# Half the products in the way back from the spectrum, x with its second half reversed throughout, and another order of first loads, fold and gates

## The chip, the cores and the metric

The kernel runs on one core of a Trainium2 chip. TensorE (PE) multiplies matrices, VectorE (DVE), ScalarE (ACT) and GpSimd (POOL) work on tiles element by element, and SyncE (SP) issues the DMAs. The metric is the device time of one launch in microseconds (us), median of several runs. Everything is float32, and each float32 matrix product stands in the profile as two records of PE.

## What is computed

Two layers of a gated cross-attention stack, for x and ctx of shape (8, 256, 1024):

```
x += tanh(g_xattn[0]) * autocorrelation(layernorm(x), ctx, ctx)      # 8 heads, top 11 lags
x += tanh(g_ffn[0])   * (LN(x) @ W.T + b + LoRA of a gated rank)     # ranks 8, 16, 32, 64
x += tanh(g_xattn[1]) * GQA(LN(x), ctx, ctx, mask)                   # 32 query, 8 key heads, rope
x += tanh(g_ffn[1])   * (LN(x) @ W1.T + b1 + 0.5 * Fourier update)

autocorrelation: corr = ifft(fft(q) * conj(fft(k))).real   over the 256 positions, per channel
  w, lag = top_k(corr, 11); w = softmax(w)
  out[t] = sum_i w_i * v[min(lag_i + t, 255)]
```

The values of the autocorrelation are thus another correlation, of v with the sparse weights, in which positions past the end count as the last one. The kernel does it with transforms of length 512 for v, 256 for the scores.

## The kernel before

The eight samples go in two passes of four (`NPASS`, `BP`). A pass holds its x as eight tiles of 128 positions by 1024 (`xt`) and takes them through all four parts; out is stored tile by tile at the end of `fourier_ffn`. The larger matrix products are made of seven products of half blocks in place of eight (`SEVEN`, `left_operands`, `right_operands`, `combine`), from operands that are sums and differences of blocks; in pass 0 they are made on chip and stored to DRAM (`wk_d`, `w0_d`, `w1_d` and others), later they are loaded.

Autocorrelation (`autocorrelation`) goes over 8 steps of a pass, a sample and half of the channels (512) each. `loads` brings the context in halves, its last row (`end`), and the second half of x reversed (`xr`, a second copy of the input). `sums` normalizes x and forms sums and differences of the position pairs (n, 255 - n), for x (`qe`, `qo`) and context (`ke`, `ko`). `normalize` forms the statistics; those of the second half are turned around by a product with a reversing matrix (`flip`, L406), since `xr` is reversed and `xt` is not. `turn` interleaves one step's forward half with the previous step's backward half: cosine and sine products (`dft`, L416), products of spectra on VectorE and their sums on GpSimd (`products`), the correlation (L563), the lags on VectorE (`lags`), and, for the previous step, the transforms of the weights, `er`, `ei` (even frequencies), `odr`, `odi` (odd), and `back` (L528): for each of the two position tiles four products with `inv2` added up in one PSUM tile, `po`, then one `residual` (L364) on VectorE that adds `tg * po` to x. The pool of `pt` and `po` (`ps_out`) has one buffer.

Between these stand steps of another generator (`beside`, run by `fill`): `keys_values` makes keys and values of the pass from ctx, 56 steps of four products for each 512 rows, and in pass 0 `fold_last_layer` then adds the Fourier update to W1. Eight steps run before the autocorrelation begins, 104 within, what is left after. Their big tiles come from two groups of seven buffers of 4 KB per partition, `ga` and `gb`: in pass 0 `ga` holds key and value weights (later all of the fold's tiles), `gb` the context (later, with `ga`, the weight `w0`). In `keys_values`, for the first 512 rows, `weight` loads four raw blocks at a unit's start, makes the sums (first unit on VectorE, the rest on GpSimd through `Short`) and stores four of them after the unit.

The fold multiplies the coefficients by a Fourier matrix (L295), and then in four rounds loads two raw W1 tiles (`w1in`), adds the update (L313, L320), forms the sums (`t12`, `t47`) and stores all to `w1_d`.

`lora_ffn` takes pairs of tiles: `prepare` normalizes and transposes a tile, multiplies it by the LoRA and gate matrix `ag` (L616), picks the rank in small VectorE operations, and transposes the result `xa` (`px`, L637); `left` forms the operands; `project` runs the seven products for the previous pair. `attention` and `fourier_ffn` follow.

The instructions of all engines are put in order ahead of time by a scheduler, which goes by the order of the program and by when it takes inputs and buffers to be free; each engine then works in its fixed order. SP's DMAs wait in that order too.

## Time and profile before

| | us |
|---|---|
| median of 3 runs (3470.31 to 3475.52) | 3472.91 |
| profiled execution | 3473.84 |
| its span | 3471.7 |
| VectorE busy | 2209.5 |
| GpSimd busy | 1412.9 |
| mean granted clock of TensorE | 0.984 |

The span is from the first to the last instruction. A line of the timeline has the start, the duration, engine, source line, operation, output and inputs, the count, and in brackets the idle time before it and what ended it. A wait line has the waiting engine and line, what it waited for, the total in us, how often and the longest. DMA issues are SP's.

### The profile page before, as it was taken

The page shows a single profiled execution, that of the slowest core. Times are in us where ns is not written, and L with a number is a line of the kernel's source. Part 1 is how long each engine was busy: PE and PEld are TensorE (multiplying, and loading weights), DVE is VectorE, ACT ScalarE, POOL GpSimd, SP SyncE. Part 2 cuts the span into 40 slices and gives each one's busy share as a digit, 9 for nine tenths or more (in the row PEclk, how much of TensorE's full clock was granted, in tenths as well). Part 3 has the DMA queues.
Part 4 walks back from the last instruction along what each step waited for, and adds up shares of the span by engine and source line. Part 5 has one row for each costly group of instructions (what it writes and reads, how often), then busy time and mean ns, then how long its engine had stood idle before and what let it go on. Part 6 is the DMA issues. An engine that isn't in the chain of part 4 may idle for free. (4 is left out here: it accounts for less than half of the span.)

```text
span 3471.7 us, 37174 instructions
## 1 busy us (share of the span) xinstructions
PE 3372.3 (97%) x12888; PEld 2303.4 (66%) x12888; DVE 2209.5 (64%) x4149; ACT 860.4 (25%) x2065; POOL 1412.9 (41%) x1259
## 2 busy tenths in 40 slices
PE   6999979999999999999999999999999999999999
PEld 4666634876777677676456666467776777777654
DVE  7667455777777766666548674456666666666662
ACT  2222101222223232223113321113222222222220
POOL 4655213244344334434545552224344344344343
PEclk8999979999999999999999999999999999999999
DMA  6343551433333333344153434043333333333411
GB/s 234 130 142 113 180 179 54 167 138 134 136 136 120 126 119 121 123 134 138 55 201 119 151 112 158 0 158 112 119 117 123 115 121 120 118 124 121 152 49 49
DMA packets 164169, 435.66 MB, mean 125 GB/s; under 512 B 21604, under 2 KB 56676, under 8 KB 163982
## 3 DMA queue, kind: packets, MB, share of 16 engines
q1 hardware_dynamic: 163982, 433.29, 37.4%
q8 instruction: 102, 1.67, 0.2%
q14 instruction: 85, 0.70, 0.1%
HBM read 354.59 MB, written 78.64 MB: 125 GB/s over the span
## 5 line engine op out<-in xcount | busy, mean ns | idle before, releaser
L699 POOL TENSOR_TENSOR qT<-rope,rope 128x512 f32<-128x512 f32 x128 | 170.0, 1328 | 865.4 <-DVE rope L698 865.4
L928 PE MATMUL po<-wo,oT 128*128 128x512 f32 x960 | 432.1, 593 | 0.0
L899 PE MATMUL ps_q<-xn,wq 128*128 128x256 f32 x1920 | 428.9, 379 | 0.0
L364 DVE SCALAR_TENSOR_TENSOR x<-po,tg,x 128x512 f32<-128x512 f32 x360 | 258.4, 745 | 231.9 <-PE po L928 70.6
L899 PEld LDWEIGHTS ps_q<-xn,wq 128*128 128x128 f32 x1920 | 364.8, 190 | 50.5 <-PE po L669 0.5
L961 ACT ACTIVATE s<-s,nmx 128x256 f32<-128x256 f32 x512 | 256.0, 501 | 275.7 <-DVE nmx L958 275.2
L956 DVE COPY_PREDICATED s<-keep,ps_s 128x512 f32<-128x512 uint8 x256 | 186.1, 730 | 182.3 <-PE ps_s L947 178.8
L928 PEld LDWEIGHTS po<-wo,oT 128*128 128x128 f32 x960 | 177.4, 190 | 175.6 <-issue 170.5
L928 PE MATMUL po<-wo,oS 128*128 128x512 f32 x640 | 287.7, 592 | 0.3 <-DVE x L364 0.3
L899 PE MATMUL ps_q<-xn_t,wq 128*128 128x256 f32 x1280 | 285.6, 379 | 0.0
L988 ACT COPY wT<-pt 128x512 f32<-128x512 f32 x256 | 138.0, 590 | 516.3 <-PE pt L982 516.3
L899 PEld LDWEIGHTS ps_q<-xn_t,wq 128*128 128x128 f32 x1280 | 243.2, 190 | 33.1
L993 PE MATMUL av<-wT,v 128*128 128x256 f32 x1024 | 247.1, 384 | 2.9 <-ACT wT L988 2.9
L947 PE MATMUL ps_s<-kT,qT 128*128 128x256 f32 x1024 | 248.3, 380 | 0.0
L993 PEld LDWEIGHTS av<-wT,v 128*128 128x128 f32 x1024 | 191.9, 190 | 78.0 <-issue 44.0
L970 DVE TENSOR_SCALAR s<-s,tot 128x256 f32<-128x256 f32 x512 | 219.6, 469 | 7.7
L955 POOL MEMSET s<- 128x512 f32 x256 | 129.8, 526 | 222.9 <-PE pt L982 221.1
L252 POOL TENSOR_TENSOR x<-x,part 128x512 f32<-128x512 f32 x80 | 115.0, 1437 | 255.1 <-ACT part L251 255.1
L696 DVE TENSOR_TENSOR rope<-c,tab 128x512 f32<-128x512 f32 x160 | 116.4, 728 | 154.0 <-POOL c L234 147.3
L928 PEld LDWEIGHTS po<-wo,oS 128*128 128x128 f32 x640 | 118.9, 190 | 136.7 <-issue 128.9
L947 PEld LDWEIGHTS ps_s<-kT,qT 128*128 128x128 f32 x1024 | 191.9, 190 | 25.5 <-DVE x L364 0.5
L958 DVE TENSOR_REDUCE nmx<-s 128x2 f32<-128x512 f32 x256 | 175.0, 685 | 8.3
(260 smaller groups left out, 5673.5 us busy)
## 6 DMA issues: line engine op xcount, KB each, us to landing
wq<-in_wq_dram SPq DMA_DIRECT2D x104, 512.0 KB, 3.4
wo<-in_wo_dram SPq DMA_DIRECT2D x104, 512.0 KB, 3.4
wq<-wq_d SPq DMA_DIRECT2D x96, 512.0 KB, 3.3
wo<-wo_d SPq DMA_DIRECT2D x96, 512.0 KB, 3.2
w<-w_d SPq DMA_DIRECT2D x36, 512.0 KB, 4.8
wk<-in_wk_dram SPq DMA_DIRECT2D x26, 512.0 KB, 5.1
wv<-in_wv_dram SPq DMA_DIRECT2D x26, 512.0 KB, 3.9
wk<-wk_d SPq DMA_DIRECT2D x24, 512.0 KB, 4.4
```

Of the source, the lines that this page charges most:

```text
L364: nc.vector.scalar_tensor_tensor(xs, ps, g, xs, ALU.mult, ALU.add)
L699: nc.gpsimd.tensor_add(dst, t0, t1)
L899: nc.tensor.matmul(ps[:, l, :], wops[r][:, l, c, :], xo[r][:, c, :], start=(c == 0), stop=(c == KH - 1),)
L928: nc.tensor.matmul(po, ops[r][:, h, t * P : (t + 1) * P], wops[r][:, h, :], start=(h == 0), stop=(h == 1),)
L947: nc.tensor.matmul(ps[:, t, :], qT[i, n][:, l, t * P : (t + 1) * P], kT[:, n * S : (n + 1) * S], start=True, stop=True,)
L955: nc.gpsimd.memset(s, MASKED)
L956: nc.vector.copy_predicated(s, keep[b], ps)
L958: nc.vector.tensor_reduce(nmx, s, AX.X, ALU.max, negate=True)
L961: nc.scalar.activation(s[:, t, :], s[:, t, :], AF.Exp, bias=nmx[:, t : t + 1], accum_out=tot[:, t : t + 1],)
L970: nc.vector.tensor_scalar(s[:, t, :], s[:, t, :], tot[:, t : t + 1], None, ALU.mult)
L988: nc.scalar.copy(wT[i], pt)
L993: nc.tensor.matmul(av[:, i, :], kv[step][1][:, n * 2 + c, :], wT[i][:, c, :], start=(c == 0), stop=(c == 1),)
```

## The change

- x comes in, and stays, with its second half of positions reversed in every sample; so do the mask's rows and the query side's rope table (`tab_q`). `xr`, `flip` and the turned statistics go. On the way out the second tile of each sample is scattered to its rows by an indirect DMA of GpSimd, through row numbers `rows`; the first is stored by SP as before.
- Position n's pair is now 255 - n for x, but the context is paired with one shift (n - 1 with 255 - n, `front`), so that the value correlation has a part that is the same for both positions of a pair and one that is opposite. `back(0)` makes the shared part from `er` and `odi`, `back(1)` the opposite one from `ei` and `odr`: two products each; each result goes to both tiles, the second time with `tg` or `ntg`. The context transforms have own matrices (`KCE` and so on), and one more product (`NYQ`) for each step.
- Loads: matrices, first context, `inv`, `inv2` and two x tiles come ahead of the other six x tiles (`late`). In pass 0, 1 + 6 steps of `keys_values` run ahead of the statistics and 7 after them; in pass 1, 1 + 4 and 3.
- `raw_weight` loads the next unit's blocks after the fourth of the seven products of a unit, just after its stores; the second `wk` unit's sums go to VectorE.
- The fold takes `w1in` from the other group (`gb`). `w0` is asked for after `ag` and `bl`.
- In `lora_ffn` the gates' transposes (`turned`) come after two steps of the previous projection; `xa` and `xaT` have four buffers.

```diff
@@ load_constants
         nc.sync.dma_start(tab, a["rope"])
+        nc.sync.dma_start(tab_q, a["rope_q"])
+        nc.sync.dma_start(rows, a["rows"])
@@ fold_last_layer
-                wt.append(big_tile(group, [2, HALF], "w1in"))
+                wt.append(big_tile(wt_group, [2, HALF], "w1in"))
@@ autocorrelation
-        mats = c1.tile([P, 4, P], F32, name="mats")
+        mats = c1.tile([P, 9, P], F32, name="mats")
         nc.sync.dma_start(mats, a["dft"])
-        inv = c1.tile([P, 2, S], F32, name="inv")
-        nc.sync.dma_start(inv, a["dft_inv"])
-        inv2 = c1.tile([P, 4, S], F32, name="inv2")
-        nc.sync.dma_start(inv2, a["lag_inv"])
-        flip = c1.tile([P, P], F32, name="flip")
-        nc.sync.dma_start(flip, a["flip"])
...
-            ps = ps_cor.tile([P, S], F32, tag="cor", name="ps_turn")
-            nc.tensor.matmul(ps[:, 0 : n * 2], flip, flat, start=True, stop=True)
...
             for b in range(n):
-                norms[b0 + b] = lin[:, b * 2, :], turned[:, b, :]
+                norms[b0 + b] = lin[:, b * 2, :], lin[:, b * 2 + 1, :]
-
-        normalize(0, 1)
...
-                kr_ps, ki_ps = dft(CE, ke), dft(SE, ko)
+                kr_ps, ki_ps = dft((KCE, ke)), dft((KSE, ko), (NYQ, ke))
...
-                vr_ps, vi_ps = dft(CO, ko), dft(SO, ke)
+                vr_ps, vi_ps = dft((KCO, ko)), dft((KSO, ke))
...
                     po = ps_out.tile([P, HALF], F32, tag="out", name="po")
-                    for k, sp in enumerate((er, ei, odr, odi)):
-                        nc.tensor.matmul(
-                            po, inv2[:, k, l * P : (l + 1) * P], sp, start=(k == 0), stop=(k == 3)
-                        )
-                    residual(b_tiles[l][:, b_cols], po, tg_x[0])
+                    for i, (k, sp) in enumerate(((0, er), (3, odi)) if l == 0 else ((1, ei), (2, odr))):
+                        nc.tensor.matmul(po, inv2[:, k, :], sp, start=(i == 0), stop=(i == 1))
+                    residual(b_tiles[0][:, b_cols], po, tg_x[0])
+                    residual(b_tiles[1][:, b_cols], po, ntg_x[0] if l else tg_x[0])
                     fill(1)
...
-        this, before = sums(*loads(order[0])), None
+        first = loads(order[0])
+        inv = c1.tile([P, 2, S], F32, name="inv")
+        nc.sync.dma_start(inv, a["dft_inv"])
+        inv2 = c1.tile([P, 4, P], F32, name="inv2")
+        nc.sync.dma_start(inv2, a["lag_inv"])
+        late()
+        fill(6 if p == 0 else 4)
+        normalize(0, 1)
+        this, before = sums(*first), None
+        fill(7 if p == 0 else 3)
@@ lora_ffn
+                return xnT, xa
+
+            def turned(xnT, xa):
                 px = ps_s.tile([R0 + 1, P], F32, tag="s", name="px")
                 nc.tensor.transpose(px, xa, ident)
...
-                got = left(m, prepare(m * 2, norm), prepare(m * 2 + 1, norm))
-                if pending is not None:
-                    project(*pending)
-                elif make_w0:
+                got = [prepare(m * 2 + i, norm) for i in range(2)]
+                steps = project(*pending) if pending else iter(())
+                for _ in range(2):
+                    next(steps, None)
+                got = left(m, *(turned(*x) for x in got))
+                if pending is None and make_w0:
                     w0.update(make_w0())
+                for _ in steps:
+                    pass
@@ keys_values
+        def raw_weight(kind, u):
             w = [[big_tile(gw, [KC * P], f"{kind}_{i}{k}") for k in range(2)] for i in range(2)]
...
+        def made_weight(kind, u, w):
             s = [big_tile(gw, [KC * P], f"{kind}_s{i}") for i in (1, 2, 4)]
             if cops:
-                ops = left_operands(Short(nc.gpsimd), w, *s)
+                eng = Short(nc.gpsimd if kind == "wv" else nc.vector)
+                return left_operands(eng, w, *s)
...
+                if n == 0 and r == SEVEN[3]:
+                    for d, k in zip(kept, (5, 7, 6, 3)):
+                        nc.sync.dma_start(d, ops[k])
+                    if u < 3:
+                        coming = raw_weight(("wk", "wv")[(u + 1) // 2], (u + 1) % 2)
                 yield
-            for d, t in later:
-                nc.sync.dma_start(d, t)
-            later.clear()
@@ attention, queries
-                        rope(qT[done[1]], done[0], tab[:, 0, :], tab[:, 1, :], w1)
+                        rope(qT[done[1]], done[0], tab_q[:, 0, :], tab_q[:, 1, :], w1)
@@ fourier_ffn
-                for i in range(2):
-                    r0 = (p * TT + m * 2 + i) * P
-                    nc.sync.dma_start(out[r0 : r0 + P, :], xt[m * 2 + i])
+                b = p * BP + m
+                nc.sync.dma_start(out[b * S : b * S + P, :], xt[m * 2])
+                nc.gpsimd.indirect_dma_start(
+                    out,
+                    bass.IndirectOffsetOnAxis(ap=rows[:, b : b + 1], axis=0),
+                    xt[m * 2 + 1],
+                    None,
+                )
@@ flamingo_kernel
-                    yield from fold_last_layer(ga, (kw1, ps_kv))
+                    yield from fold_last_layer((ga, gb), (kw1, ps_kv))
...
-            for t in range(TT):
-                r0 = (p * TT + t) * P
-                nc.sync.dma_start(xt[t], a["x"][r0 : r0 + P, :])
-            for _ in range(7):
-                next(steps)
+            load_x(range(2))
...
-        if p == 0:
-            w0, make_w0 = {}, ffn_weight(nc.vector, (gb, ga), lambda k, j: a["w0"][k, j])
...
                 nc.sync.dma_start(bl, a["bl"])
+                if p == 0:
+                    w0, make_w0 = {}, ffn_weight(nc.vector, (gb, ga), lambda k, j: a["w0"][k, j])
@@ _layout
-        "x": i["x"].reshape(B * S, D),
-        "xr": i["x"][:, : P - 1 : -1].reshape(B * P, D),
-        "ctx": turned(i["ctx_4096"]).reshape(B * S, D),
+        "x": turned(i["x"]).reshape(B * S, D),
+        "ctx": paired.reshape(B * S, D),
```

## The prediction

> **What bounds it now.** I read the busy shares first, then the busy time by stretch, then who waited for whom, then the timeline at the longest waits.
>
> ```profile
> PE 3372.3 (97%) x12888; PEld 2303.4 (66%) x12888; DVE 2209.5 (64%) x4149; ACT 860.4 (25%) x2065; POOL 1412.9 (41%) x1259
> ```
>
> TensorE (PE) sets the end: only 99 us of 3471.7 are without a matmul. So a removed matmul counts in full wherever PE has no gap, and a removed gap counts too. The busy time by stretch (columns: width, then busy us and instructions of PE, weight loads, VectorE, ScalarE, GpSimd; granted clock; DMA share; GB/s) shows where gaps lie:
>
> ```profile
> 40.00:200.00 160.00, 132.76 (x456) 90.92 (x457) 106.72 (x242) 44.90 (x82) 105.80 (x80) 0.89 0.46 155
> 200.00:410.00 210.00, 208.52 (x804) 148.05 (x803) 134.03 (x343) 55.32 (x100) 101.55 (x81) 1.00 0.41 131
> 410.00:500.00 90.00, 72.44 (x200) 31.38 (x199) 49.91 (x103) 6.48 (x14) 5.59 (x4) 0.77 0.67 231
> ```
>
> PE is full at clock 1.00 in 200 to 410 us (autocorrelation of pass 0), and loses time at the start and in the fold (410 to 500), partly to a lower clock. PE's waits (total us, times, longest):
>
> ```profile
> PE acc L313 <- DVE w1in L320: 15.1, 3, 6.3
> PE px L637 <- DVE xa L635: 12.0, 7, 1.8
> PE ps_k L774 <- POOL wk_s L152: 9.4, 1, 9.4
> ...
> PE pa L616 <- DMA ag<-in_ag_dram: 6.8, 1, 6.8
> ...
> PE ps_turn L406 <- ACT cor L566: 4.0, 1, 4.0
> ```
>
> Nearly half of the 99 us stand in these five lines, and each of the five instructions is touched by the change.
>
> **Reverse transform: products removed.** The chain has the price of a product:
>
> ```profile
> 2099.96 3.43 PE po L532 x8
> ```
>
> Eight records are the four products of one `back`: each float32 product is two records, so 0.86 us. A turn drops from 8 products to 4, and gains one (the Nyquist row, `NYQ`). With 16 turns (2 passes x 4 samples x 2 column halves): 16 x 3 x 0.86 = 41.3. The flip products of the statistics go too (8 records, 1.5 us busy, hidden in part): 0.7. Together **-42**.
>
> VectorE gets two more `residual` per turn: 32 x 0.745 = 23.8 us (mean of its group). Its cover is the PE-bound stretch, where it is busy 134 of 210 us, so nothing is charged; with the cover gone it would cost up to 23.8. But order matters. Turn five of pass 0:
>
> ```profile
> 281.27 1.72 POOL L438 TENSOR_TENSOR odi<-ma,mb 128x512 f32<-128x512 f32 x1
> 281.61 1.02 PE L532 MATMUL po<-odr,inv 128*128 128x512 f32 x2
> 283.05 1.12 PE L532 MATMUL po<-odi,inv 128*128 128x512 f32 x2 [0.43 <-POOL odi L438]
> 288.40 0.74 DVE L364 SCALAR_TENSOR_TENSOR x<-po,tg,x 128x512 f32<-128x512 f32 x1
> 289.20 1.13 PE L532 MATMUL po<-re,inv 128*128 128x512 f32 x2
> ```
>
> `odi`, the last thing GpSimd makes, was the fourth product; in the new `back(0)` it is the second, 1.7 us sooner. Here it ends at 282.99 and would be wanted at 280.75: 2.2 us of wait. The same subtraction in all 16 turns gives 12.7 (three turns of each pass with 0.9 to 2.4, the rest near nothing), 0.7 of it there already: +12. PE is in order, so the fill and next transposes queue behind. `po` has one buffer, now held for two residuals: in the same turn the second `back` started 0.06 us after the residual, so 0.74 more lands on PE, in four turns or so: +2. I take **+14**; ends 0 (other products are placed between) and +25.
>
> **First loads.** Pass 0 now loads two x tiles, the matrices and the first context before the other six x tiles, runs 14 key steps instead of 8 ahead of the first turn, loads the second raw key weights in the middle of the previous unit, and makes them on VectorE instead of GpSimd. Moved on SP's queue: six x loads behind `cn`, `end`, `inv`, `inv2`; four stores and four raw loads before the next `cn`, the last raw loads holding SP until a key product is done. `tab_q` and `rows` are two small loads more; the `xr` loads (16 x 256 KB) go. Stretch 40 to 200 holds 119 us of work at back-to-back spacing (0.43 us per record of 512 columns, in proportion to columns), so 41 are lost. Removable: the wait on `wk_s` 9.4 and the half-speed records behind it 1.9 (8 records 3.78, elsewhere 1.89); `ke` 3.8 and half-speed transforms behind 2.6; `re`, `im`, `kn`, the raw load 6.2 and 1.5 behind. That is 25. What stands in the way is VectorE: 106.7 busy, plus 8 half-operations of 0.68 (5.4) and 3 us of residuals, is 115 in a stretch that would be 160 - 25 - 10 = 125. GpSimd falls from 105.8 to about 94. At 92% VectorE would be the next thing late, with key products waiting on its evictions; the two `ps_v` waits (3.3 and 5.5, both on VectorE) stay. I take **-17**; ends -3 and -25.
>
> Here a rule weighs. The Trainium skill, TensorE: Matmul & The Clock Gate, section Part 1: The HAM clock gate (the "warmup" mystery), says that PE falls to half clock after an idle window of about 3.4 us and needs as long to come back, some 1.7 us lost for each. By the rule gaps under 3.4 lose nothing extra; the row after a 3.29 us gap (8 records in 3.68 us, at 133 us) lost 1.8, and one of 1.99 lost 1.0. I go by the rows. By the rule the half-speed terms would be 1.7 each behind `ke`, `wk_s` and (below) `ps_turn`, and none behind `re` and `im`: 4 us less to remove, a sum of -72 instead of -76.
>
> **Fold of the last layer.** The eight raw w1 tiles were loaded into the same buffers as the results that wait to be stored:
>
> ```profile
> 451.44 1.90 SPq L308 DMA_DIRECT2D w1in<-in_w_dram  x2
> 457.81 7.19 PE L313 MATMUL acc<-dec,encr 40*128 40x512 f32 x8 [5.62 <-DVE w1in L320]
> 464.84 1.92 SPq L308 DMA_DIRECT2D w1in<-in_w_dram  x2
> ```
>
> 13.4 us a round. In the other group, empty after the last key product, the loads can run ahead, and a round is VectorE's 8 operations of 0.69, about 5.5 to 6: three rounds save 22. The price: of the eight half-loads of the first FFN weight (`w0`, 0.5 MB each) six had come by 412 us; they want that group and now follow the w1 stores: 4.2 MB at the 400 GB/s of the best slices is 10.5 us, partly under the last round, then VectorE's sums; I charge 9. **-13**; ends 0 and -22.
>
> **Gates.** `turned` moves behind two steps of the previous projection (6.9 us), longer than the VectorE chain that `px` waits for. Seven waits, 12.0 us; the first (1.24) has no projection ahead of it and stays: **-10** (ends -5, -11).
>
> **Pass 1's start and FFN.** `ag` no longer follows the weight loads: 6.8, plus half-speed records (16 in 3.65 instead of 1.9), with `xn` ready in 1.6 us anyway: **-7** (ends -3, -8.5). Without the flip the 4.0 us `ps_turn` wait goes, and about 3 of half-speed transforms behind it; the next thing late is VectorE's `top`: **-5** (ends -2, -7).
>
> **Stores.** Every second output tile leaves by a scatter on GpSimd's queue, which is not in the trace. Behind it stand the next-but-one sample's operand sums, wanted 24 us later: nothing. At the end it counts:
>
> ```profile
> 3465.42 3.11 SPq L1111 DMA_DIRECT2D out_dram<-x  x2
> 3467.42 0.75 DVE L364 SCALAR_TENSOR_TENSOR x<-po,tg,x 128x512 f32<-128x512 f32 x1 [2.02 <-PE po L1101]
> ```
>
> The second tile goes at 3465.4 and the first at 3468.2, landing 2.6 us later (last column of the DMA issues, with the count and the size before it):
>
> ```profile
> out_dram<-x SPq DMA_DIRECT2D x8, 512.0 KB, 2.6
> ```
>
> If the scatter runs freely it ends no later: 0. If it is ordered behind the plain store, because both write `out`, another landing follows: 2.6 by the row. A rule speaks against the change: the Trainium skill, SBUF — State Buffer, section SBUF: two separate sides, says of its "DVE blocks DMA" trap that descriptors written by GpSimd wait while VectorE holds the shared port, 0.62 us becoming 3.1. That would make it 5.7; VectorE is idle here, so I go near the row, with some generation time: **+4** (ends 0, +6).
>
> **Sum.** -42 + 14 - 17 - 13 - 10 - 7 - 5 + 4 = -76. The profiled execution took 3473.84 (span 3471.7 and 2.1 around it), 0.9 above the median of 3472.91; 76 off the one and the other gives 3397.8 and 3396.9. **Predicted 3398**, own range 3380 to 3415.
>
> **Rivals.**
> - Chance 0.27: the products go but the stalls only move. VectorE is already near full before 200 us, and `w0` comes late: start -5, fold 0, turn -4, scatter +6, the rest as above: -48, **3425** (3412 to 3445). For it: VectorE's 92%. Against it: DMA idles in many slices of the fold.
> - Chance 0.20: stalls go wholly and the order of products lets PE pass `odi`: -42 + 3 - 25 - 22 - 11 - 8 - 7 + 0 = -112, **3361** (3350 to 3375). For it: the four-product turns at 103 and 197 us wait for nothing. Against: 0.06 us of slack at 289.
> - Chance 0.04, slower: the single `po` buffer. If both residuals stand behind a pair of `lags` (4 us of VectorE) in every `back`, PE waits there. The rest of the sum is -90, over 32 `back`s: it decides from 2.8 us each; at 3.5 the time is 3473 + 22 = **3495**. Against it: only two of 32 waited, 0.75 each.
> - Chance 0.01: no change that can be told; the product count alone speaks against that.
>
> **Numbers.** The likeliest has 0.48. Within 0.2% (7 us) is about what a measurement of this kernel can't tell from no change. 3358 to 3440 leaves out the slower case, the ends of the two others and little of the likeliest. Faster 0.95, same 0.01, slower 0.04.
>
> **What would show it.** The reverse transform's records fall from 256 to 128. Right: no `px`, `ps_turn`, `ag` or `wk_s` in the waits; `po <- odi` with about 12 us; w1 rounds near 6 us; the span's end set by the scatter. Wrong: `po` waiting on residuals in most turns, PE below 0.95 at 40 to 200 us on VectorE, or a project step waiting for `w0`.

## The result and the profile after

The changed kernel took **3440.88 us** (median of 4 runs, 3440.27 to 3441.86), the kernel before 3474.22 beside it: a ratio of **0.9904, 95% interval 0.9887 to 0.9921**, so 33 us less. The forecast was 3398, 76 less; 3440.88 lies 0.88 us above 3440, the upper end of the wider of the two ranges given with it.

The busy shares of the changed kernel first (engine, busy us, share, instructions), then its busy time by stretch, with the same columns as before:

```profile
PE 3335.6 (97%) x12784; PEld 2287.7 (67%) x12784; DVE 2227.5 (65%) x4181; ACT 860.5 (25%) x2061; POOL 1413.8 (41%) x1259
```

```profile
40.00:200.00 160.00, 134.70 (x499) 96.92 (x498) 112.22 (x269) 45.13 (x81) 95.94 (x73) 0.89 0.44 155
200.00:397.00 197.00, 190.11 (x730) 133.79 (x730) 137.19 (x345) 55.01 (x99) 98.07 (x77) 0.99 0.43 140
397.00:475.00 78.00, 71.10 (x184) 33.58 (x183) 49.74 (x106) 7.47 (x15) 6.21 (x5) 0.76 0.62 222
```

PE is busy 37 us less, and idle about as long (3438.5 - 3335.6 = 103 us; 99 before). The middle stretch, full before (208.5 of 210), now has 7 us without a product in 197. The waits of PE say what came in place of those that went:

```profile
PE po L531 <- POOL odi L434: 18.1, 8, 5.4
PE po L531 <- POOL re L432: 11.7, 4, 9.2
PE px L647 <- DVE xa L642: 10.4, 6, 1.7
...
PE pa L623 <- ACT xnT L367: 4.3, 1, 4.3
...
PE po L670 <- DMA w<-in_w_dram: 3.6, 1, 3.6
...
PE po L670 <- DVE w_t L140: 2.9, 1, 2.9
```

`wk_s` on GpSimd, `w1in`, `ps_turn` and `ag` are gone from the list. In their place the reverse transform (`po`, L531) waits 29.8 us, `px` kept 10.4 of its 12.0, and the first projection waits for `w0` (its tiles `w` and sums `w_t`). The timeline of turn five, to compare with the one before:

```profile
274.28 1.27 POOL L434 TENSOR_TENSOR odi<-ma,mb 128x512 f32<-128x512 f32 x1
275.60 1.25 PE L531 MATMUL po<-odi,inv 128*128 128x512 f32 x2 [2.56 <-POOL odi L434]
277.82 1.39 DVE L371 SCALAR_TENSOR_TENSOR x<-po,tg,x 128x512 f32<-128x512 f32 x2
```

Here `po` waits 2.56 us where 2.2 was forecast. The first turn (106 us) was far worse: 9.2 and then 5.4 us, where the forecast had at most 2.4 for any turn. Without these two waits 15.2 us are left in all turns, near the 12.7 forecast. The cause in the first turn stands in three engines' timelines put together:

```profile
90.06 2.49 POOL L154 TENSOR_TENSOR wv_s<-wv,wv 128x512 f32<-128x512 f32 x2
92.52 2.48 POOL L158 TENSOR_TENSOR wv<-wv,wv 128x512 f32<-128x512 f32 x2
...
99.86 1.27 POOL L240 TENSOR_TENSOR c<-w,m 128x512 f32<-128x512 f32 x1
101.16 0.69 DVE L712 TENSOR_TENSOR rope<-c,tab 128x512 f32<-128x512 f32 x1 [12.10 <-POOL c L240]
...
105.91 2.08 PE L531 MATMUL po<-re,inv 128*128 128x512 f32 x2 [9.24 <-POOL re L432]
```

GpSimd works through sums of the raw value weights (`wv_s`, `wv`) before a key combination (`c`); VectorE, in order, stands 12.1 us for that `c` with the spectra's multiplications behind it; so `re` is late and PE stands. In the kernel before, the same sums came behind the first reverse transform, which began at 103.45 us and waited for nothing:

```profile
108.85 2.95 POOL L148 TENSOR_TENSOR wv_s<-wv,wv 128x512 f32<-128x512 f32 x2 [6.70 <-PE ps_k L774]
```

For the steps below I cut the span at seven places and compare each part. **Lost** is, as in the prediction, a part's length less its records at back-to-back spacing (0.43 us for 512 columns). Kernels that differ from this one only behind the last Fourier product (L302) reach it between 399.3 and 404.3 us; so I read nothing below 5 us out of this first part. The medians of the kernel before, beside the different runs, lie from 3471.76 to 3475.38; so I read nothing below 4 us out of two medians alone.

| part | before | after | |
|---|---|---|---|
| start to last Fourier product | 426.0 | 403.6 | -22.5 |
| to first projection of the LoRA FFN | 49.8 | 39.5 | -10.3 |
| to attention | 138.7 | 144.6 | +5.9 |
| to the keys of pass 1 | 1170.9 | 1169.8 | -1.1 |
| to the last reverse transform of pass 1 | 361.9 | 355.2 | -6.7 |
| to attention of pass 1 | 155.3 | 152.2 | -3.1 |
| to the last product | 1164.7 | 1164.7 | 0.0 |
| to the end of the span | 4.3 | 9.0 | +4.6 |

### The profile page after: what moved, and what is told of

Its sections match the earlier page's. It is cut to its first block, busy times and chain, and to the rows that moved or that the text cites. A ratio compares the mean times of both kernels' runs of the same rounds, so it can differ in the third digit from the quotient of the medians.

```text
span 3438.5 us, 36954 instructions
## 1 busy us (share of the span) xinstructions
PE 3335.6 (97%) x12784; PEld 2287.7 (67%) x12784; DVE 2227.5 (65%) x4181; ACT 860.5 (25%) x2061; POOL 1413.8 (41%) x1259
## 3 DMA queue, kind: packets, MB, share of 16 engines
q8 instruction: 102, 1.67, 0.2%
## 5 line engine op out<-in xcount | busy, mean ns | idle before, releaser
L371 DVE SCALAR_TENSOR_TENSOR x<-po,tg,x 128x512 f32<-128x512 f32 x376 | 268.8, 745 | 227.1 <-PE po L950 70.6
L258 POOL TENSOR_TENSOR x<-x,part 128x512 f32<-128x512 f32 x80 | 114.8, 1435 | 196.4 <-ACT part L257 196.4
L263 POOL TENSOR_TENSOR x<-x,part 128x512 f32<-128x512 f32 x80 | 102.9, 1287 | 166.9 <-DVE part L371 143.7
```

The costliest lines, as they stand in the source:

```text
L371: nc.vector.scalar_tensor_tensor(xs, ps, g, xs, ALU.mult, ALU.add)
```

## The experiments

All start from the changed kernel; times are medians beside the kernel before on the same chip, and "longer" or "less" is against 3440.88.

**1. Gates in place.** `turned` goes back into the place where its products stood.

```
- got = [prepare(m * 2 + i, norm) for i in range(2)]
+ got = left(m, *(turned(*prepare(m * 2 + i, norm)) for i in range(2)))
  steps = project(*pending) if pending else iter(())
- for _ in range(2):
-     next(steps, None)
- got = left(m, *(turned(*x) for x in got))
```

> The changed kernel with the gates' transposes back in their old place in the program (turned right after each prepare, the previous projection whole behind them). Theory: the place in the program does not set when px runs. The second pair's xnT waits for one of its two buffers, which project's fourth of its own blocks frees, so the second pa, and with it px, comes just ahead of the next projection either way. Then the six waits of px of 1.7 us stay and the time is that of the changed kernel (0.990 of the kernel before) within 2 us. Rival: the move brought its part of the gain; then px waits come to 12 us or more in seven places and the time is 3 to 10 us longer than the changed kernel's.

Measured: 3446.68 (ratio 0.9924, 0.9908 to 0.9941), 5.8 longer; `px` waits 10.2 us in six, 1.70 each. So the waits are set as the theory says, not by the place in the program; but the time doesn't agree with it. What is longer lies ahead of the first `px` that waits in each pass, that of the second pair (1.6 us to the first projection and 2.5 behind it in pass 0, 2.7 in pass 1); from there one waiting `px` follows another after 35.19 us here and 35.13 in the changed kernel. Why this first stretch of each pass was shorter with the move was not taken apart.

**2. Four buffers for `xnT`.**

```
- xnT = w2.tile([P, KC, P], F32, tag="xnT", name="xnT")
+ xnT = w2.tile([P, KC, P], F32, tag="xnT", name="xnT", bufs=4)
```

> The changed kernel with four buffers for xnT in the LoRA FFN in place of two. Theory: the two buffers of xnT hold the second pa back until just ahead of the next projection; with four, pa comes earlier, px has the projection's products between, and the six waits of 1.7 us go: 10 us less than the changed kernel (0.9876 of the kernel before). Rival: VectorE's chain behind pa, stretched while GpSimd makes the left operands, makes px late wherever it stands; then waits of px of 1 to 2 us stay and the time falls by 0 to 3 us.

Measured: 3428.99 (0.988, 0.9864 to 0.9897), **11.9 less**. No line of `px` on `xa` is left among the waits; the projections to attention take 11.1 us less and the FFN of pass 1 6.1 less, the stretch ahead of the first projection 5.2 more. In pass 1 the second pair's `pa` start at 2127.5 and 2129.2 us, and in the changed kernel at 2137.1 and 2151.0. The theory stands: what held `px` was the buffer of the operand (`xnT`) of the product `pa` ahead of it. In the changed kernel ScalarE's copy into that buffer waits for products of the projection, and `pa` follows it at 2150.98 us:

```profile
2150.35 1.07 ACT L367 COPY xnT<-pt 128x512 f32<-128x512 f32 x2 [12.84 <-PE po L670]
```

**3. Reverse transforms swapped.** `back(1)` (`ei`, `odr`) goes first, `back(0)` second.

```
- back(0)
+ back(1)
  cor += correlation(re, im, 2)
...
- back(1)
+ back(0)
```

> The changed kernel with the two reverse transforms of a turn in the other order: the opposite part (ei, odr) first, the shared part (er, odi) second. GpSimd makes er, ei, odr, odi in this order, so the last is asked for some 10 us of PE's work later. Theory: it is this order that costs. The waits of po on re and odi (29.8 us in the changed kernel, 0.7 before) fall to under 12, hardly any on odr comes in their place, and the time falls by 12 to 20 us (0.985 to 0.987). Rival: GpSimd's queue as a whole is late in the turns concerned, since sums of the value weights and of the keys stand in it ahead of the spectra; then most of the wait moves to odr or im and the time falls by less than 6 us.

Measured: 3434.83 (0.989, 0.9873 to 0.9906), 6.0 less, at the edge of the rival. The sum of the waits falls to 20, but the first turn waits even longer than 9.2, now for `ei` (the profile names its buffer, `im`).

```profile
PE po L531 <- POOL im L434: 19.8, 6, 10.5
```

**4. Each product of the reverse transform made twice** (values of this part doubled). This prices the products taken out.

```
- for i, (k, sp) in enumerate(((0, er), (3, odi)) if l == 0 else ((1, ei), (2, odr))):
-     nc.tensor.matmul(po, inv2[:, k, :], sp, start=(i == 0), stop=(i == 1))
+ (k0, s0), (k1, s1) = ((0, er), (3, odi)) if l == 0 else ((1, ei), (2, odr))
+ for i, (k, sp) in enumerate(((k0, s0), (k0, s0), (k1, s1), (k1, s1))):
+     nc.tensor.matmul(po, inv2[:, k, :], sp, start=(i == 0), stop=(i == 3))
```

> The changed kernel with each of the two products of a reverse transform made twice, so four in a row as before (values doubled in this part of x; odi is asked for 1.7 us later). 64 products of 0.86 us are added. Theory: a product costs its full price where PE has no gap, and in the other turns fills the wait for odi; 55 us less the 10 to 15 us of waits that it covers: 40 to 46 us longer than the changed kernel, 1.002 to 1.0035 of the kernel before. Rival: the turns are bound by the spectra of VectorE and GpSimd, so that the products taken out were for a good part hidden; then 15 to 30 us longer.

Measured: 3469.13 (0.9991, 0.9982 to 1.0), only **28.3 longer** for 64 products that cost 55: the rival holds. Half of what was taken out had been hiding something. Waits of `po` on GpSimd are 17.0 here, 12.8 less than in the changed kernel:

```profile
PE po L532 <- POOL re L432: 10.4, 2, 9.3
...
PE po L532 <- POOL odi L434: 6.6, 5, 3.8
```

The waits of `pt` on GpSimd and of the key and value products on VectorE fall by some 5. About 9 of the 27 are left. They go with the clock: in these two parts of the span (start to the last reverse transform of pass 0, first key product to the last reverse transform of pass 1) PE's granted clock is at half for 27 us in all here and for 51 in the changed kernel. The middle of pass 1's autocorrelation, this kernel and then the changed one:

```profile
1943.00:2073.00 130.00, 125.08 (x473) 87.15 (x473) 97.82 (x229) 36.35 (x67) 70.38 (x57) 1.00 0.32 107
```

```profile
1930.00:2060.00 130.00, 120.75 (x448) 84.73 (x447) 100.23 (x232) 36.07 (x66) 66.02 (x52) 0.95 0.33 109
```

Lost time, from the start to the last reverse transform of pass 0, is 61.0 before, 45.6 here and 59.4 in the changed kernel; in pass 1 from its first key product 12.5, 13.3 and 26.8. So the start of pass 0 gained 15 by this reading, and taking out products gave back 13.8 and 13.5. In pass 1 no weights' sums stand on GpSimd; there the loss comes without them.

**5. Raw w1 tiles back among the results.** In the fold `wt_group` becomes `group` again.

> The changed kernel with the raw w1 tiles of the fold back in the group of the results (the fold's part of the change undone alone). Theory: the other group makes the rounds about 10 us shorter in sum, but the raw tiles stand where w0 is to come, and 6 of the 10 are given back as a later w0 (the waits of 3.6 and 2.9 us in the first projection). Then this kernel is 3 to 6 us longer than the changed one, has acc waiting on w1in again, and no wait of the first projection for w0 or its sums. Rival: w0 is late because it is asked for after ag and bl; then the waits for w0 stay and the time is 9 to 13 us longer.

Measured: 3445.28 (0.9919, 0.9902 to 0.9936), 4.4 longer, as the theory has it: 9.9 us longer to the first projection, where `acc` waits for `w1in` again, and 5.7 shorter in the projections, without a wait for a load of `w0`.

```profile
PE acc L320 <- DVE w1in L327: 12.4, 3, 6.2
```

**6. Value weights' sums on VectorE.** `Short(nc.gpsimd if kind == "wv" else nc.vector)` becomes `Short(nc.vector)`.

> The changed kernel with the sums of the raw value weights (8 half-operations for each of two units) on VectorE in place of GpSimd. Theory: they stand in GpSimd's queue ahead of a key combination, on which VectorE waits 12 us in order (89 to 101 us), and so ahead of re, im, odr, odi of the first turns; without them the waits of po of 9.2 and 5.4 us at 106 and 113 us go or fall below 2, and the time falls by 9 to 15 us. Rival: VectorE, busy 69 of 90 us from 40 to 130, is then the next thing late, key and value products wait for its evictions, and the time falls by less than 4 us.

Measured: 3437.66 (0.9899, 0.9882 to 0.9915), 3.2 less, no more than the noise. The first turn's waits fall as expected, though not below 2:

```profile
89.46 3.44 DVE L158 TENSOR_TENSOR wv<-wv,wv 128x512 f32<-128x512 f32 x2
98.84 1.12 PE L531 MATMUL po<-re,inv 128*128 128x512 f32 x2 [3.73 <-POOL re L432]
102.97 2.07 PE L531 MATMUL po<-odi,inv 128*128 128x512 f32 x2 [3.00 <-POOL odi L434]
```

So the sums cause the larger part of that wait (14.6 us, 6.7 here). The time does not fall by the 7.9 us that went: in their place `po` waits 2.1 for a residual, and the half-operations (each on half a tile's columns) take VectorE up to 1.7 us while GpSimd works, not 0.68.

**7. Scatter ahead of the plain store** in the program.

```
- nc.sync.dma_start(out[b * S : b * S + P, :], xt[m * 2])
  nc.gpsimd.indirect_dma_start(...)
+ nc.sync.dma_start(out[b * S : b * S + P, :], xt[m * 2])
```

> The changed kernel with the scatter of a sample's second tile ahead of the plain store of its first tile in the program. Theory: the scatter waits for the plain store to land, since both write out; its own tile is ready 2.8 us before the other, so in this order it runs at once, and the plain store follows when it has landed: from the last product to the end 5 to 6.5 us in place of 9.0, 3 us less in all. Rival: the scatter's own time to landing is what costs (4.7 us for the last); then the plain store ends as late, 8 to 10 us after the last product, and the time stays.

Measured: 3438.43 (0.99, 0.9883 to 0.9916), 2.4 less, which alone would say nothing; but from the last product to the end it is 5.3 us in place of 9.0. The two tails, this kernel's first:

```profile
3429.41 0.98 POOL L1132 DMA_INDIRECT out_dram<-x,rows  x1 [5.24 <-DVE x L371]
...
3432.80 0.33 SPq L1138 DMA_DIRECT2D out_dram<-x  x1
```

```profile
3429.58 0.75 DVE L371 SCALAR_TENSOR_TENSOR x<-po,tg,x 128x512 f32<-128x512 f32 x1 [2.02 <-PE po L1123]
3433.77 0.97 POOL L1133 DMA_INDIRECT out_dram<-x,rows  x1 [11.16 <-DMA out_dram<-x]
```

In the changed kernel the scatter stands until the plain store has landed; here it leaves as soon as its tile is ready, 5.9 us sooner when counted from the last product.

**8. One raw w1 tile of each round in either group**: `big_tile(wt_group if k else group, ...)`.

> The changed kernel with one raw w1 tile of each round of the fold in the group of the results and one in the other group, so that four, not eight, of them stand where w0 is to come. Theory: w0 is late because its buffers hold raw w1 tiles; with three of them free from the start its loads come sooner, the waits of the first projection (3.6 on the load, 2.9 on its sums) go or halve, and the rounds stay as short: 3 to 6 us less. Rival: the results' group is what limits the rounds, so acc waits on w1in again; then 2 to 6 us longer.

Measured: 3440.7 (0.9911, 0.9895 to 0.9928), no difference. The wait for `w0`'s load went, and `acc` waits 7.4 us on `w1in` again: +7.7 to the first projection and -5.8 behind it. Each theory is right in its half: buffers given to one use are taken from the other.

**9. A step of keys or values moved ahead of the correlation**, from behind the first reverse transform.

```
- fill(3 if last else 1)
+ fill(3 if last else 2)
...
-     fill(1)
+     fill(l)
```

(`l` is 0 in the first reverse transform of a turn and 1 in the second.)

> The changed kernel with one key or value step of each turn (8 records, 1.7 us of PE) moved from behind the first reverse transform to ahead of the correlation, so that both reverse transforms come 1.7 us later behind the same spectra. Theory: the products taken out of PE's order were the time in which VectorE and GpSimd made the spectra; a step of other work in their place covers up to 1.7 us of each of some 12 waits: the waits of po on re and odi fall from 29.8 to 14 to 18 us and the time falls by 10 to 14 us. Rival: the turns go at the pace of GpSimd and VectorE, and the wait only moves (to the correlation, to pt on both, to key products on VectorE); then the time falls by less than 4 us.

Measured: 3448.99 (0.9932, 0.9916 to 0.9949), **8.1 longer**. My theory fell. The waits on `re` and `odi` went from 29.8 to 17.9 as it said, and others came:

```profile
PE po L531 <- POOL odi L434: 10.4, 3, 5.4
...
PE po L531 <- DVE x L371: 7.8, 3, 4.1
PE po L531 <- POOL re L432: 7.5, 1, 7.5
...
PE pt L515 <- POOL both L552: 5.7, 3, 3.4
...
PE ps_k L794 <- DVE v L244: 5.0, 1, 5.0
PE ps_v L794 <- DVE c L244: 4.7, 1, 4.7
```

With the two transforms close together, the second finds the one buffer of `po` held by two residuals (7.8 us): the mechanism of the slower rival, which the list of waits of the changed kernel does not show. `pt` and the key and value products wait for what VectorE and GpSimd have not done yet. Here a wait of PE was moved, not filled.

**10 to 12, 16. The start undone**: the loads and steps ahead as before (10), the second key unit's sums on GpSimd (11), the raw loads after a whole unit (12), and all three (16).

```
10:
- load_x(range(2))
+ load_x(range(TT))
+ for _ in range(7):
+     next(steps)
...
- lambda: load_x(range(2, TT)),
+ lambda: None,
...
- fill(6 if p == 0 else 4)
- fill(7 if p == 0 else 3)
11:
- eng = Short(nc.gpsimd if kind == "wv" else nc.vector)
+ eng = Short(nc.gpsimd)
12: the stores of `kept` and `raw_weight` of the next unit
- after the unit's fourth product
+ after its seventh
```

> The changed kernel with the first loads and the steps ahead as before (all eight x tiles first, 1 + 7 steps ahead of the first turn, none behind the statistics, both passes); the raw weights' place and the second key unit's sums on VectorE stay as changed. Theory: most of the 15 us gained in the first 400 us comes from the key weights' sums, so undoing the loads gives back 3 to 6 us there, and in the second pass 0 to 3. Rival: the order of loads is what gained; then 10 to 16 us longer, with ke or the first transforms late again.

Measured: 3447.17 (0.9924, 0.9907 to 0.994), 6.3 longer, but nothing of it before the last Fourier product (403.0): 4.9 in the fold and the projections, where the first two `px` wait 5.8 us in place of 0.4, and some 2 in pass 1. Neither theory placed it there. What stands before the last Fourier product is an exchange: `wk_s` comes 4.3 us late, now from VectorE, and a value product waits 5.1 us for VectorE; but the value weights' sums stand behind the first turn's spectra again (98.25 us), and that turn's `po` waits 0.9 us, not 14.6:

```profile
96.18 1.12 PE L531 MATMUL po<-odi,inv 128*128 128x512 f32 x2 [0.91 <-POOL odi L434]
```

So it is the order of first loads and steps that brought these sums ahead of the first turn.

> The changed kernel with the second key unit's sums back on GpSimd; all else as changed. Theory: the wait for them (9.4 us before) and the half-speed products behind it come back for the larger part, 6 to 11 us longer. Rival: the raw blocks come so much earlier now (after the fourth product of the unit before) that GpSimd makes the sums in time; then within 3 us, and a part of VectorE's load is lifted.

Measured: 3442.36 (0.9914, 0.9898 to 0.9931): the rival holds; there is no wait on GpSimd's `wk_s`.

> The changed kernel with the raw key and value weights loaded, and the made ones stored, after a whole unit of keys or values as before, in place of after its fourth product. Theory: neither the order of the first loads nor the engine of the sums gained alone; what is left is the earlier place of the raw loads. Then 8 to 15 us are given back within the first 400 us, with key products waiting on wk_s. Rival: with 14 steps ahead of the first turn the sums would be in time in any case, each of the three edits being enough alone; then within 4 us.

Measured: 3441.55 (0.9909, 0.9894 to 0.9924): the rival holds again.

> The changed kernel with all three edits of the start undone at once (the loads and steps ahead as before, the raw weights loaded after a whole unit, the second key unit's sums on GpSimd). Theory: each of the three is enough alone to have those sums in time, which is why undoing one gave nothing back in the first 400 us; undone together, key products wait 6 to 10 us for wk_s again and 8 to 15 us are given back: 1.0 to 4.2 us per thousand, so 0.9935 to 0.996 of the kernel before with what undoing the loads alone cost (6 us) in it. Rival: the gain in pass 0's start came from what this leaves in place (no flip product, no second copy of x to load); then it is within 4 us of the kernel with the loads undone (0.9924).

Measured: 3452.68 (0.9945, 0.9928 to 0.9961), 11.8 longer, 7.4 of it before the last Fourier product. The old waits are back:

```profile
PE ps_k L792 <- POOL wk_s L158: 10.9, 1, 10.9
...
PE dft L412 <- DVE ke L467: 6.2, 1, 6.2
```

So with any two of the three edits the wait of 10.9 does not come (4.3 is left in 10, nothing of the second unit's in 11 and 12), and each, undone singly, looks worth little or nothing in the first 400 us.

**13. One addition to x in place of two** behind each reverse transform: the other tile of the pair goes without.

```
- residual(b_tiles[0][:, b_cols], po, tg_x[0])
- residual(b_tiles[1][:, b_cols], po, ntg_x[0] if l else tg_x[0])
+ b_x = b_tiles[l][:, b_cols]
+ residual(b_x, po, tg_x[0])
```

> The changed kernel with one addition to x for each reverse transform in place of two: the one to the other tile of the pair is left out (32 operations of 0.74 us on VectorE, 23.8 us). Theory: VectorE sets part of the turns' pace once PE has fewer products, so its two more operations a turn are no longer hidden: the waits of po, pt and of the key and value products on VectorE fall by 8 us or more in sum, and the time falls by 8 to 14 us. Rival: the waits come from when GpSimd gives the spectra, not from VectorE's load; then the time falls by 0 to 4 us, and po waits on re and odi as before.

Measured: 3434.93 (0.989, 0.9875 to 0.9906), 6.0 less, between theory and rival; `po` still waits 27.3 us on GpSimd. So VectorE's 24 us of further additions cost some 6; most of the new waits are not theirs.

**14. `xn` of the LoRA FFN in other memory**: `big_tile("xn", [D], "xn")`. It follows a chain at the start of pass 1 in the changed kernel:

```profile
2119.27 0.81 DVE L356 TENSOR_SCALAR xn<-x,mv,rstd 128x1024 f32<-128x1024 f32 x1 [3.41 <-DMA v_d<-v]
...
2120.43 0.29 ACT L351 ACTIVATE rstd<-mv,eps 128x2 f32<-128x2 f32 x1 [11.04 <-DVE mv L350]
2120.64 1.05 ACT L367 COPY xnT<-pt 128x512 f32<-128x512 f32 x2
2121.26 3.68 PE L623 MATMUL pa<-ag,xnT 128*128 128x68 f32 x16 [4.26 <-ACT xnT L367]
```

> The changed kernel with the normalized tile xn of the LoRA FFN in a buffer of the group that the autocorrelation's products used, not in the memory that held the last values' tile. Theory: in pass 1 VectorE waits 3.4 us for the store of that tile before it can write the second xn, the statistics and so ScalarE's copies of xnT stand behind it in order, and pa behind these; without it the 4.3 us of pa go or fall under 1.5, and the wait of pt on xn (7.5 in two) falls too: 3 to 8 us less. Rival: ag comes no sooner than that (its load follows the same stores); then pa waits for ag in its place and the time falls by less than 2 us.

Measured: 3443.51 (0.9914, 0.9899 to 0.993), no less. The rival holds: two things come late at the same time, and with one away the other is waited for.

```profile
PE pa L623 <- DMA ag<-in_ag_dram: 3.2, 1, 3.2
```

**15 and 17. Edits together**: four `xnT` buffers, value weights' sums on VectorE, scatter first, and the swapped transforms (15) or not (17).

> The changed kernel with four of the edits together: four buffers for xnT, the reverse transforms swapped, the raw value weights' sums on VectorE, the scatter ahead of the plain store. Theory: they touch different waits (12, 6, 3 and 2 us alone), the two in the turns of pass 0 in part the same one: 18 to 23 us less than the changed kernel, 0.984 to 0.9855 of the kernel before. Rival: the turns' pace takes back what the two edits in them gain; then 12 to 15 us, 0.9862 to 0.987.

Measured: **3421.29** (0.9847, 0.9834 to 0.986), 19.6 less than the changed kernel; the four gave 11.9, 6.0, 3.2 and 2.4 alone.

> The combined kernel with the reverse transforms in the changed kernel's order again (four buffers for xnT, value weights' sums on VectorE, scatter first). Theory: the swap and the sums on VectorE take away the same first wait, so the swap brings little beside them: 1 to 5 us longer than the combined kernel (3421), so 3422 to 3426. Rival: the swap is worth its 6 us in the other turns too; then 3427 or more.

Measured: 3421.03 (0.9853, 0.9837 to 0.987). Beside the others the swap brings nothing that can be told.

**18. The fold's operands on 128 partitions.** What made me look is the busy time by stretch in the fold of the changed kernel:

```profile
403.50:407.50 4.00, 4.00 (x10) 1.37 (x9) 2.95 (x6) 0.59 (x1) 0.00 (x0) 1.00 0.43 131
407.50:414.00 6.50, 6.50 (x19) 3.13 (x18) 4.80 (x8) 1.10 (x2) 0.00 (x0) 0.66 0.67 253
414.00:420.00 6.00, 6.00 (x14) 3.21 (x15) 2.49 (x4) 0.07 (x1) 0.00 (x0) 0.50 0.31 119
```

PE has no idle time, and its granted clock falls from 1.00 to 0.50 all the same. It stays at 0.50 to the first projection, and VectorE, taken as the bound of a round, is busy 24 of 39 us:

```profile
403.55:443.00 39.45, 39.04 (x91) 19.22 (x90) 24.39 (x56) 3.46 (x7) 0.00 (x0) 0.58 0.54 193
```

```
- encr = big.tile([R1, D], F32, tag=group, name="encr")
- nc.sync.dma_start(encr, a["encr"])
+ encr = big.tile([P, D], F32, tag=group, name="encr")
+ nc.gpsimd.memset(encr, 0.0)
+ nc.sync.dma_start(encr[0:R1, :], a["encr"])
...
- dec = big.tile([R1, D], F32, tag=group, name="dec")
+ dec = big.tile([P, D], F32, tag=group, name="dec")
+ nc.gpsimd.memset(dec, 0.0)
...
- dec[:, h * HALF : (h + 1) * HALF], accs[h][0:R1, :], AF.Copy, scale=0.5
+ dec[0:R1, h * HALF : (h + 1) * HALF], accs[h][0:R1, :], AF.Copy, scale=0.5
```

> The changed kernel with the fold's two operands encr and dec on 128 partitions in place of 40, the other 88 filled with zeros by GpSimd (same sums, same number of products). In the changed kernel PE is busy for 39.0 of the 39.4 us of the fold's rounds, but its granted clock falls from 1.00 to 0.50 at about 411 us without any idle time before, and stays there to the first projection. Theory: products of 40 of 128 rows count as too little activity for the clock; with 128 rows it stays above 0.8, a record of 512 columns takes 0.43 us and not 0.94, the stretch from the last Fourier product to the first projection falls from 39.5 us to 25 to 33 us or VectorE's chain takes over, and the time falls by 3 to 10 us. Rival: the clock falls for another reason (waits too short to be listed, the narrow products beside them, the work before); then it stays near 0.58 and the time within 3 us.

Measured: 3428.3 (0.9865, 0.9849 to 0.9882), **12.6 less**; from the last Fourier product to the first projection 27.3 us in place of 39.5. Two stretches and a line of records of this run come first, then a line of records of the changed kernel:

```profile
400.00:410.00 10.00, 9.66 (x37) 5.12 (x37) 8.70 (x16) 1.17 (x2) 0.00 (x0) 1.00 0.59 218
410.00:420.00 10.00, 9.78 (x43) 5.52 (x41) 9.31 (x23) 1.07 (x2) 0.00 (x0) 1.00 0.87 330
404.99 1.88 PE L322 MATMUL acc<-dec,encr 128*128 128x512 f32 x4
```

```profile
418.04 3.78 PE L320 MATMUL acc<-dec,encr 40*128 40x512 f32 x4
```

Four records take half the time, at a granted clock of 1.00, and VectorE is busy 18 of 20 us: now it is the bound that the prediction took it for, at some 5.2 us a round (four from 399.3 to 420.0). The transposes and the narrow products between the records are in both kernels, so they alone did not lower the clock. The kernel with this and the edits of 17 was not run.

## Why the prediction was wrong

Its sign held, and the direction of all terms but one (the start of pass 1); most sizes were too large. Two steps failed most: the +14 for new waits behind the removed products, which came to 27, and the round of the fold, which took 9 us and not 6. Numbers under "by", and in brackets below, are those of the experiments.

| step of the sum | forecast | measured | by |
|---|---|---|---|
| products less new waits, -42 + 14 | -28 | about -14 | 4, with 13.8 for `NYQ` (16 x 0.86, an estimate) |
| first loads | -17 | -12 | 16; 7.4 of it before the last Fourier product |
| fold | -13 | -4 | 5 |
| gates | -10 | -6 | 1; 1.6 of it in `px` |
| `ag` | -7 | -2.5 | 6.8 to 4.3 in the waits; 14 |
| start of pass 1 | -5 | about 0 | 4: lost 13.3 against 12.5 |
| stores | +4 | +4.6 | tails |

These add to -34, near the -33 measured; but `ag` and pass 1's start are read from waits, not undone alone, and each other edit was undone with the rest in place, so the agreement is partly luck.

- **Products and new waits.** The products went as counted (128 records, 256 before). The failed term is the +14: new waits and the half clock behind them took 27, just above the +25 of its upper end. It was worked out by subtracting 1.7 us in turns that were taken to be as before. For the waits of `po` this came out near: they are 12.8 us more than in 4, against +12. What the sum had at nothing was the rest: some 5 us in waits of other products for VectorE and GpSimd, which had been working under the removed products, and some 9 (what is left of the 27) with the clock at half. The 14.6 us of the first turn are a matter of the first loads: in 4 they are 13.1. "Nothing is charged" for the two more residuals was wrong by up to 6 (13), perhaps a part of the same 27.
- **First loads.** Near in size, wrong in place. The wait for `wk_s` went, yet from 40 to 130 us no less is lost (28.4 before, 30.7 after): the stall moved to the first turn's `re` and `odi` (14.6 us), since the new order had put the value weights' sums into GpSimd's queue ahead of them (6 and 10), a cost that the sum did not have. What was gained lies from 130 to 200 us (12.9 lost before, 4.1 after), at the two `ps_v` waits of which I had said that they stay (a wait of 3.0 now stands at 309 us).
- **Fold.** The raw tiles do run ahead and the waits on `w1in` go. The failed step is "a round is VectorE's 8 operations": it was taken at full clock, while PE at half clock is slower than VectorE, so that a round takes some 9 us, not 5.5 to 6. The profile of before already showed 7.19 us for 8 records. With 18 the clock stays up and a round takes 5.2. That `w0` comes late was foreseen at 9 and took 5.7 (5).
- **Gates.** "Longer than the VectorE chain" holds for the order in the program. On the engine `pa` itself had to wait until the previous projection had read `xnT` and so released it, and `px` followed it there as before; with more buffers (2) both came early.
- **`ag` and pass 1's start.** "`xn` ready in 1.6 us anyway" looked at the first tile. Before the change, too, the second tile waited 3.5 us for the store of a value tile in its memory, and ScalarE's copies stood behind it. In place of `ps_turn` (4.0) `pt` waits 1.8 for `both` on GpSimd and a key product waits 1.5; the `top` on VectorE that the prediction named is not waited for.
- **Stores.** Right, and by the mechanism named: the scatter is ordered behind the plain store (7). The trap that the prediction weighed did not show: the last scatter took 0.97 us on GpSimd, and the eight of them landed after 3.9 us (median).

The rival "products go but the stalls only move" was the nearest in kind, and the measured time lies in its range (3412 to 3445); but it, too, kept +14, and got there by smaller gains at the start and in the fold. Of the signs of error that the prediction named, one came in full: a projection step waits for `w0`. PE is busy for 0.84 of the stretch from 40 to 200 us, but its longest waits there are for GpSimd.

## What to carry over

Work taken from the bounding engine is worth its price only where the others are ahead: put it back once, as in 4, to learn what it hid (27 of 55 us here). Before moving an instruction, ask which buffer holds its operand: one line for buffers gave 12 us, where the move took 1.6 off the waits and some 6 off the time. Look at the granted clock beside PE's busy share: a stretch can be full and still run at half speed.

## What was not expected of the hardware

- PE's granted clock fell from 1.00 to 0.50 at 409.6 us, with no idle time since 403.5, in products that used 40 of 128 rows, and stayed at 1.00 through the rounds when the other rows held zeros (18). The Trainium skill, TensorE: Matmul & The Clock Gate, section Part 1: The HAM clock gate (the "warmup" mystery), ties the half clock to idle windows; here busy time alone does not keep it up. What exactly is counted, rows or something that goes with them, the run does not say.
- The wait after which products run at half speed is not fixed either: in pass 1 of the changed kernel waits of 1.40 and 1.58 us (at 1826 and 1865 us) were followed by two records in 1.13 us; after waits of 1.88, 0.70 and 1.67 us within 7 us (1941 to 1948 us) two took 2.07 and 2.08. The rows that the prediction went by were nearer to this than the rule of an idle window of 3.4 us; the 1.7 us lost for each such window was an estimate, 3.4 us at half speed. In the changed kernel's trace each stretch at half clock inside the span lasts 3.4 us or a multiple of it (3.4, 6.8, 10.2, 20.5, 37.5), so a short wait that sets one off costs more than itself.
- Some of VectorE's operations stretch beside GpSimd. Of the changed kernel's VectorE operations on 512 columns with two tiles in SBUF as inputs, 50 of the 82 that met a GpSimd operation other than a memset took over 1 us, mostly 1.67; none of the 415 that met nothing did (0.69). GpSimd's own took 1.27 or, beside such an operation, often 1.72. VectorE's additions from PSUM (0.75) did not stretch.
